# A macaron block (mixture, state space, mixture) on one core: other mixture groups, results in the sorted rows, the drive product in halves, the bias as bf16, and another written order

## The chip, the cores and the metric

The kernel runs on one core of one Trainium2 chip. The time is the device time of one execution, in microseconds; less is better. Six units matter. TensorE (PE) multiplies matrices. VectorE (DVE), ScalarE (ACT) and GpSimd (POOL) work element by element. SyncE (SP) starts the transfers (DMAs) of a hardware queue, GpSimd those of a software queue, whose rows are picked by an index.

## The reference

The input is two sequences of 2048 tokens with 128 features. Three steps are added to it in turn. A "mixture" is a mixture of 32 experts, four for each token, plus a shared network; both mixtures have the same weights. The "state space" is a selective scan with 256 channels and 16 states.

```python
x = x + 0.5 * _L0_ffn_ref(_layernorm(x, axis=-1), ...)
x = x + _L0_attn_ref(_layernorm(x, axis=-1), ...)
x = x + 0.5 * _L0_ffn_ref(_layernorm(x, axis=-1), ...)

# mixture
scores = softmax(flat @ router_w.T + router_bias)
topk_scores, topk_idx = jax.lax.top_k(scores, 4)          # then normed to a sum of 1
h = silu(einsum('nd,ehd->neh', flat, gate_w)) * einsum('nd,ehd->neh', flat, up_w)
expert_out = einsum('neh,edh->ned', h, down_w)
out = (sel * topk_scores[:, :, None]).sum(axis=1)         # sel: the four chosen
out = out + silu(flat @ sgate_w.T) * (flat @ sup_w.T) @ sdown_w.T

# state space
x_proj, z = split(x @ W_in + b_in, 2);  u = silu(x_proj)
Bm, Cm = split(u @ W_x + b_x, 2);       dt = softplus(u @ W_dt + b_dt)
def step(h, inp):
    h = h * exp(dt_t[..., None] * A) + (dt_t * u_t)[..., None] * B_t[:, None, :]
    y_t = einsum('bds,bs->bd', h, C_t) + D_param * u_t
    return (h, y_t)
return (y * silu(z)) @ W_out + b_out
```

## The kernel before

The 4096 tokens are eight blocks of 512 (four tiles of 128 each), blocks 0 to 3 for one sequence and 4 to 7 for the other. Everything is in fp32 unless said otherwise.

**State space.** Blocks go one after the other (`state_space`, L1281). A block's opening works out u, z, B, C, dt and dt times u (`dtu`). Then there are 16 states, each with these steps. SP spreads a row of B over the partitions (`bs`). GpSimd multiplies `dtu` by it into `hst`, both halves of the channels (2 x 512) in one instruction (`drive`, L1456). ScalarE makes two decays `da` (`decay`, L1468). TensorE spreads a row of C (`c`, L1480). VectorE runs two scans in place on `hst`, one for each half (`scan`, L1494), and multiplies by C (`times_c`, L1507). TensorE adds the transposed result to `y` (L1271). Four `hst` buffers are in turn. At the end of a block `project` (L1566 to 1584) multiplies by W_out; its first matmul for each tile has a single row of ones (`ones_row`) against the row of the bias (`bout`), both fp32.

**Mixture.** `mixture(li, gi)` (L649) does one group of blocks of a layer. Layer one has the groups (0), (1), (2, 3) and (4, 5, 6, 7); layer two has (0, 1, 2, 3), (4, 5), (6) and (7). VectorE's routing finds for each token its four experts and a row for each choice, so that rows of one expert lie together in tiles of 128. GpSimd scatters the normed tokens to these rows in DRAM (`scatter`, L916, one DMA for a tile and a choice). Then the experts work on a "quad", four tiles at a time. SP loads the rows (`xs`) and the weights (`wt`), TensorE transposes (L1066), multiplies by gate and up (`gate_up`, L1076) and down (`down_q`, L1104), ScalarE copies and applies silu, VectorE multiplies, and SP stores the results (`ys`). GpSimd gathers each token's four results (`gather`, L1197), TensorE sums them with their weights (`weighed`, L1230), VectorE adds the sum to x.

A group works on a fixed number of tiles, `SURE`: 32, 48 or 80 for one, two or four blocks; so a layer has 8 + 8 + 12 + 20 = 48 quads. Tiles beyond that are worked in a branch (`more`) only where the routing needs it. A group of one block has one tile for each expert, so its weights are the experts in order: it reads them from the inputs in three pieces, gate, up and down (`take`, L1016), and the first group also writes them out side by side (`lay`) as `w_dram`. Larger groups take each tile's weights from `w_dram` by the routing's list (`fetch`, L1038). Sorted rows lie in one DRAM buffer for each size of group, results in others, two for each size used in turn. All are cleared with zeros at the start (`clear_rows`, L466): rows fully, results beyond the fixed tiles. That is 52 and 24 stores of 256 KB.

**Order.** Each step is an operation with an engine, a list of buffers read and written, and a function that emits its instructions. `ORDER` (L47) is a written list of the numbers of these operations; the kernel emits them in exactly this order, and each engine runs its own in the order of emission. So an engine that waits at one operation holds up all its later ones. ScalarE's activation tables are loaded where the next operation in the order needs the other set (`tables`, L413). On GpSimd, from the third of a row of scatters or gathers on, a small memset (`pause`, L408) stands ahead of each.

Of the kernel before, what the change touches and what calls it, by code (L numbers as in the profile page):

```python
# [8 lines left out]
F32 = mybir.dt.float32  # L9
# [21 lines left out]
SURE = {1: 32, 2: 48, 4: 80}  # L31
# [4 lines left out]
GROUPS = (((0,), (1,), (2, 3), (4, 5, 6, 7)), ((0, 1, 2, 3), (4, 5), (6,), (7,)))  # L36
# [11 lines left out]
0 10 108-112 20 113 9 19 2 528 8 3 529 114-120 14 121 123 21 23 25 16 24 15 17-18 530-531 31 1 122 124-125 22 126-128  # L48
131 27 132-133 537 532 29 533 326 538-539 134 534-535 11 129-130 536 41 540-544 135 148 150 144 149 146-147 143 145
142 140 139 141 170 13 12 151 153 545-548 138 549 34 37 327 35 39 32 137 551 328 186 550 552-553 152 155 28 554 26 154  # L50
202 136 171 329 156-157 38 218 36 188 40 30 555 158 33 558 159 161 160 162 169 163-165 556 330 166-167 559 185 557 201
331 174-175 594 560 168 190 596 6 191 176-177 187 172 561 217 206 332 233 207 178 333-335 595 179 597 336-337 180-181
338 222 4 192 182 223 193-194 183 208-209 195-196 204-205 211 857 212 197 265 210 219 339 224 340 213 225 5 226 342
598 341 343 599-600 173 344 601 220 856 184 92 198-199 203 249 238 189 602 227 562 592 234 239 604 228-229 281 603 605
855 574 568 7 200 214 606 345 266 215 608 230 607 609 270 231 271 610 587 221 858 236 254 611 346 250 252 282 582
859-860 612 255 251 283 349 613 240 614 575 570 237 615 243 284 616 861 241-242 244 268 245 286 618 253 287 272-274
256 267 257 216 617 258 619 235 285 620-621 624 622 246 626 247 623 269 862-863 866 591 564 625 627 275 297 628 589
276-277 629 278-279 291-292 565 43 293 584 590 967 969 248 350 288-290 69 968 95 232 970-971 347-348 389 388 973 259
52 59 260 972 105 261 572 975 974 871 351 977 567 976 569 262 978 263 979 981 45 980 60 982 294 352 295 983-984
369-372 573 64 566 373 67 375 588 374 280 377 379 91 66 376 378 380 578 872 864-865 873 876 381 583 383 382 384 581  # L60
403 867 877 48 874 868 296 878 107 875 264 42 879-880 869 68 46 585 870 881-883 886 885 50 57-58 61 100 44 51 884 887
63 888 580 385 402 593 571 891 62 563 386 889 47 579 65 98 55 586 75 577 576 49 353 368 367 354 357 365-366 362 364
358-359 355 360-361 363 890 892-893 356 894-895 82 387 390-391 56 392 54 393 395-396 394 298 397 401 96 300-301
404-405 415 418 409 314 419 313 53 429 306 305 308-309 320 406 417 416 423 410-411 424 407 299 408 432-433 443 425
398-399 457 302 446 896 431 430 412-413 307 319 445 434-435 899 436 414 447 437 303 420 438-439 310 421-422 444 458
304 311 460 630 322 312 461 316 426 321 448 427 315 459 323 317 633 400 90 471 318 428 634 449-450 798 903 451-453
324-325 70 1432-1433 465-467 462 631 463 440-441 1434 464 106 635-637 454 485 101 632 455 468-469 900 473 644 474-475
917 479-481 1435-1436 638 1439 639 1440 934 442 658 472 97 645 487 640-641 913 960 642 470 486 456 488 647 489 648 952
476 102 919 477-478 1437 661 490 672 1438 928 491 646 906 923 908 493-494 662 72 914 933 492 905 499 495 675 907 922
916 926 909 912 924 659 649-651 904 932 910 686 482 676 83 652-653 927 918 931 929 921 654 94 483 936 925 915 920 911  # L70
930 961 1458 643 1459 74 1460 1452-1453 1461-1462 93 1463 1454 660 673 99 496-497 1455-1456 655 700 1441-1442 964 943
656 1445-1446 1448-1449 687 674 701 663 1450-1451 1457 680-682 664-665 715 1447 484 959 938 666 677 667-668 1466 657
688 669 678 689-690 670 679 985 1470 498 987 1468 683-684 1467 1471 703 1469 714 1472-1473 951 940 76 1464 986 988
1476 1478 704 1479 1465 728 717 1486 1496 1477 1481 691 73 1480 692-693 718 705-706 1506 694 702 1482 695-696 707 671
716 1475 1488 731-732 1489 1483 697 897 955 966 1487 898 698 742 965 729 85 708 699 709-710 79 719-720 1490 756 1491
1485 1492-1493 730 1516 721 1498 1484 757 711 1500 944 941 722 1474 712 736 1495 733 1497 1499 685 1526 1501-1503 953
939 1510 1508 737 1507 723 1504 734 724-725 735 1509 738 726 1511 942 937 745 71 743 1512 739-740 949 80 1513 758 744
759 746 1518 950 1519 1494 946 1517 956 1443 760 1521 1505 770 1522 1444 771 747 1520 989 991 1536 947 748-749 508 784
764-765 935 1527 785 766 990 954 992 962 945 750 993 995 713 727 761 751 772 762 1515 1528 1537 963 500 958 948 957
752 81 1523 763 994 753 1524 1529 786 507 1530 996 773 1531-1532 1514 741 1533 754-755 774 1538 1541 1546 775 767 776  # L80
768 1556 502 1547 1540 777 787 1539 503 501 1542 1054 1040 788 1525 1535 1548 789-791 1557 516 1543 997 1068 778-780
521 792 1545 793-794 1055 1053 999 781 1039 1550 998 1000 1067 769 1081 1534 1549 782 1551-1552 795-796 1056 1042 1057
504 1558 1041 1553 1043 1559 1058 505 1059 797 1060 783 506 1069 1061-1063 1070-1071 1082 1047 1084 1048-1049 510
1561-1562 514 523 509 1085 511 77 1566 1064-1065 1072-1074 1044-1045 1095 1075 1109 1046 1555 88 1076 1544 1083 1096
1123 522 1567 517 1568 1050 1077-1078 515 524 1051 1066 901 1079 1098-1099 1124 1560 1563 1112 1571 1576 512 1110 1089
1113 1569 1090 513 1086 1097 1126 89 799 1091 1572 1087 1565 518 1088 1570 525 1127 1100 1573 1554 1101 1577 519-520
1102 526-527 1636 1578 1637 1111 1092 1001 1137 1093 1581 1002 1114 1638 1579 1588 1115 1128-1129 1116 1103 1586 1104
1130 1639 1105 800 84 1052 1080 1117 1125 1640 78 1118 1106 86 1138 87 803 821 1094 1107 1140 1119 1141 1587 1003 1120
807 1005 806 1596 1131 820 1564 1121 1582 1591 1132-1133 1151 808 1643 1152 1139 1597 1641 1606 1574 1644 1142 1642
902 1143 1580 1134 1656 1575 1589 1135 1598 1657 1144 1136 1592 1165 1601 1004 802 1599 1583 1662 1658 1663 1607 1006  # L90
1659-1660 1166 1664 1608 1122 1661 1585 1590 1602 1593 1154 1616 1155 1179 1600 1665 1611 1666 1584 1609 1645 1153
1145 1603 1146 1180 1617 1649 1612 1147 1610 1613 1646 1193 1604 1650 1652 1108 1159 1168 822 801 1653 1651 1160 1169
# [225 lines left out]
def macaron_kernel(  # L318
# [162 lines left out]
    for (li, gi), b in results.items():  # L481
        if b.t is not None and not b.writers:
            clear_rows(b, SURE[len(GROUPS[li][gi])] // SQ)
# [1172 lines left out]
```

## Time and profile before

| | us |
|---|---|
| median of 7 runs | 1267.98 |
| lowest and highest of them | 1263.65 and 1272.78 |
| the profiled execution | 1272.94 |
| its span, first to last instruction | 1271.2 |
| busy: POOL | 973.3 |
| busy: PE | 969.2 |
| busy: DVE | 823.2 |
| busy: ACT | 784.8 |

The busy time of an engine is an average over stages with different limits, so it is read by stretches of the span. A stretch's row gives for each engine its busy time and the number of its instructions, then the granted clock of TensorE as a share, the mean busy share of the 16 DMA engines and what they moved. In the slices, each digit is the busy share of a fortieth of the span in tenths (9 is 90% or more). A row of the groups gives line, engine, operation, what is written from what, shapes and number; then the busy time of all, the mean of one in ns; then how long the engine had been idle just before them and what ended most of that. TensorE shows an fp32 matmul as two records.

### The profile page before, as it was taken

The numbers are of one execution on the slowest core, as the hardware profiler recorded it, in microseconds if no ns is written. First come the engines' busy times: TensorE is split into PE (matmuls) and PEld (weight loads), VectorE is DVE, ScalarE is ACT, GpSimd is POOL, SyncE is SP. The second block draws the span as 40 slices with busy tenths as digits, with TensorE's granted clock in tenths as the row PEclk, the third lists the DMA queues.
The fourth block names the chain that finished last, engine by engine and source line by source line (L and its number), as shares of the span: only waits on it lengthen the run. The fifth ranks groups of instructions, "written<-read, shape, count | busy, mean of one in ns | idle before, by whom it ended". The sixth has DMA issues, their size and how long they took to land. (4 is left out here: it accounts for less than half of the span.)

```text
span 1271.2 us, 19402 instructions
## 1 busy us (share of the span) xinstructions
PE 969.2 (76%) x5848; PEld 769.6 (61%) x5848; DVE 823.2 (65%) x1643; ACT 784.8 (62%) x1532; POOL 973.3 (77%) x1043
## 2 busy tenths in 40 slices
PE   3777775778798978877677665668898889778776
PEld 2556564566767767564555444446777877676664
DVE  7652452166576999899989999989788632312221
ACT  4342343576789999577879735776687737424442
POOL 3876578288858775798989879998886867588686
PEclk9998987899999999688888877989899989979997
DMA  9797767488978554222232212232788978677842
GB/s 317 228 301 242 254 199 218 152 267 279 307 215 248 152 165 145 75 66 72 82 86 64 78 45 88 95 115 82 230 263 256 293 226 260 163 214 195 218 112 68
DMA packets 253513, 226.85 MB, mean 178 GB/s; under 512 B 24513, under 2 KB 218690, under 8 KB 253378
## 3 DMA queue, kind: packets, MB, share of 16 engines
q1 hardware_dynamic: 236994, 191.67, 49.6%
q0 software_dynamic: 16384, 33.59, 9.2%
q8 instruction: 59, 0.97, 0.3%
q14 instruction: 76, 0.62, 0.2%
HBM read 154.65 MB, written 70.52 MB: 177 GB/s over the span
## 5 line engine op out<-in xcount | busy, mean ns | idle before, releaser
L1456 POOL TENSOR_TENSOR hst<-dtu,bs 128x1024 f32<-128x1024 f32 x128 | 302.3, 2367 | 58.4 <-ACT st L1519 11.2
L1197 POOL DMA_INDIRECT yg<-ys,idx x256 | 246.5, 963 | 108.1 <-PE sum L1230 39.3
L1076 PE MATMUL gu<-xT,wt 128*128 128x128 f32 x1536 | 221.7, 297 | 50.9 <-issue 23.5
L1076 PEld LDWEIGHTS gu<-xT,wt 128*128 128x128 f32 x1536 | 205.5, 210 | 82.6 <-issue 39.6
L1494 DVE TENSOR_TENSOR_SCAN hst<-da,st,hst 128x512 f32<-128x512 f32 x192 | 240.2, 1272 | 17.5 <-POOL hst L1456 8.8
L916 POOL DMA_INDIRECT xs<-xn,idx x192 | 189.4, 987 | 75.8 <-issue 38.3
L1468 ACT ACTIVATE da<-dt,a 128x512 f32<-128x512 f32 x256 | 174.8, 690 | 74.0 <-DVE hst L1494 63.5
L1094 DVE TENSOR_TENSOR h<-sgq,gu 128x256 f32<-128x256 f32 x192 | 77.9, 417 | 201.5 <-ACT sgq L1088 88.8
L1271 PEld LDWEIGHTS y<-ident,hst 128*128 128x128 f32 x1024 | 133.0, 155 | 76.2 <-issue 48.7
L415 ACT ACT_TABLE_LOAD x130 | 166.8, 1283 | 4.1 <-ACTq L1139 1.0
L1271 PE MATMUL y<-ident,hst 128*128 128x128 f32 x1024 | 149.6, 296 | 18.5 <-DVE hst L1507 17.4
L1507 DVE TENSOR_TENSOR hst<-hst,c 128x1024 f32<-128x1024 f32 x128 | 154.9, 1210 | 13.1 <-PE c L1480 5.3
L1088 ACT ACTIVATE sgq<-gu 128x256 f32<-128x256 f32 x192 | 71.1, 383 | 137.3 <-PE gu L1076 73.5
L1104 PE MATMUL oq<-wt,h 128*128 128x128 f32 x768 | 109.6, 289 | 20.0 <-issue 12.3
L1104 PEld LDWEIGHTS oq<-wt,h 128*128 128x128 f32 x768 | 100.7, 202 | 34.2 <-issue 20.3
L1480 PE MATMUL c<-cm,pick 128*128 128x512 bf16 x128 | 54.7, 428 | 79.7 <-DVE hst L1507 75.7
L409 POOL MEMSET pad<- 128x256 bf16 x336 | 110.1, 328 | 0.2
L1113 ACT COPY yq<-oq 128x512 f32<-128x512 f32 x96 | 55.7, 585 | 81.4 <-PE oq L1104 38.7
L1230 PEld LDWEIGHTS sum<-yg,dg 128*128 128x128 f32 x512 | 71.4, 209 | 38.5 <-issue 17.8
L1230 PE MATMUL sum<-yg,dg 128*128 128x128 f32 x512 | 77.9, 299 | 20.5 <-issue 11.3
L1222 ACT ACTIVATE dg<-ident,wk 128x128 f32<-128x128 f32 x256 | 80.9, 393 | 13.3 <-PE sum L1230 13.3
L1069 ACT COPY xT<-pt_x 128x512 f32<-128x512 f32 x96 | 55.8, 584 | 48.0 <-PE pt_x L1066 15.5
(154 smaller groups left out, 1519.2 us busy)
## 6 DMA issues: line engine op xcount, KB each, us to landing
wt<-w_dram SPq DMA_DIRECT2D x256, 192.0 KB
bs<-bd SPq DMA_DIRECT2D x128, 256.0 KB
xs<-xs SPq DMA_DIRECT2D x96, 256.0 KB
ys<-yq SPq DMA_DIRECT2D x96, 256.0 KB
xs<-zero SPq DMA_DIRECT2D x52, 256.0 KB
wt<-in_gate_w SPq DMA_DIRECT2D x64, 128.0 KB
wt<-in_up_w SPq DMA_DIRECT2D x64, 128.0 KB
wt<-in_down_w SPq DMA_DIRECT2D x64, 128.0 KB
```

The source lines that it names most:

```text
L409: pool(nc.gpsimd.memset(pad, 0.0))
L415: nc.scalar.preload_act_table_set(name)
L916: nc.gpsimd.indirect_dma_start(out=xs_b.t, out_offset=bass.IndirectOffsetOnAxis(ap=route["idx"][:, i * TB + t, k : k + 1], axis=0), in_=xn ...
L1076: nc.tensor.matmul(gu.t[:, j, s, :], wt.t[:, s, j * H : (j + 1) * H], xT.t[:, s0 + s, :], start=True, stop=True,)
L1104: nc.tensor.matmul(o.t[:, s, :], h.t[:, s, :], wts[s // 2].t[:, s % 2, 2 * H :], start=True, stop=True,)
L1197: nc.gpsimd.indirect_dma_start(out=yg.t[:, k, :], out_offset=None, in_=ys_b.t, in_offset=bass.IndirectOffsetOnAxis(ap=route["idx"][:, i * ...
L1230: nc.tensor.matmul(sm_.t, dg.t[:, k, :], yg.t[:, k, :], start=(k == 0), stop=(k == TOPK - 1),)
L1271: nc.tensor.matmul(y[:, t, k * P : (k + 1) * P], src[:, k, t * P : (t + 1) * P], ident.t, is_transpose=True, start=start and k == 0 and t ...
L1456: nc.gpsimd.tensor_tensor(h.t[:, :, 1:], dtu.t, bs.t.unsqueeze(1).to_broadcast([P, ND, T]), ALU.mult)
L1468: nc.scalar.activation(da.t, dt.t[:, k, :], AF.Exp, scale=a_t.t[:, k, s : s + 1])
L1494: nc.vector.tensor_tensor_scan(h.t[:, k, 1:], da.t, h.t[:, k, 1:], 0.0 if ini else st_sb[:, k, s : s + 1], ALU.mult, ALU.add,)
L1507: nc.vector.tensor_tensor(h.t[:, :, :T], h.t[:, :, 1:], cb.t.unsqueeze(1).to_broadcast([P, ND, T]), ALU.mult,)
```

## The change

It has five parts.

- Groups: layer one is (0), (1, 2, 3), (4, 5, 6, 7), layer two (0, 1, 2, 3), (4, 5, 6), (7). A group of three blocks works on 68 tiles, so a layer has 8 + 17 + 20 = 45 quads. The single group of layer two reads its weights from `w_dram` in one piece for two experts (`again`) rather than from the inputs in three.
- Results: for groups of three and four blocks they are stored over the sorted rows that they come from; only groups of one block have a buffer for results. Rows are cleared with 12 + 20 + 24 stores and results with 4.
- GpSimd's product for a state is two instructions of 512 elements, one for each half, and a scan depends on its own half.
- Bias: at the start VectorE splits it into three bf16 rows whose sum stands for the fp32 value, in partitions 0, 32 and 64 of a tile of zeros (`bo3`). In `project` a bf16 matmul of 128 rows of ones with this tile replaces the fp32 one.
- `ORDER` is another list: 4327 operations in place of 4340.

```diff
-SURE = {1: 32, 2: 48, 4: 80}
+SURE = {1: 32, 3: 68, 4: 80}
-GROUPS = (((0,), (1,), (2, 3), (4, 5, 6, 7)), ((0, 1, 2, 3), (4, 5), (6,), (7,)))
+GROUPS = (((0,), (1, 2, 3), (4, 5, 6, 7)), ((0, 1, 2, 3), (4, 5, 6), (7,)))
 ORDER = """
...
@@ buffers in DRAM
             if n not in rows:
                 rows[n] = dram_buf(f"xs{n}", [slots(blocks) * P, D])
-            same = [k for k in results if len(GROUPS[k[0]][k[1]]) == n]
-            if len(same) < 2:
-                results[li, gi] = dram_buf(f"ys{n}{len(same)}", [slots(blocks) * P, D])
-            else:
-                results[li, gi] = results[same[len(same) % 2]]
+                if n == 1:
+                    results[n] = dram_buf(f"ys{n}", [slots(blocks) * P, D])
+                else:
+                    results[n] = Buf(t=rows[n].t)
...
-    for (li, gi), b in results.items():
-        if b.t is not None and not b.writers:
-            clear_rows(b, SURE[len(GROUPS[li][gi])] // SQ)
+        if n == 1:
+            clear_rows(results[n], SURE[n] // SQ)
...
+    bo3 = kept("bo3", [P, D], BF16)
+
+    def parts():
+        left = const.tile([1, D], F32, tag="bo_left", name="bo_left")
+        nc.vector.memset(bo3.t, 0.0)
+        nc.vector.tensor_copy(bo3.t[0:1], bout.t)
+        nc.vector.tensor_tensor(left, bout.t, bo3.t[0:1], ALU.subtract)
+        mid = const.tile([1, D], BF16, tag="bo_mid", name="bo_mid")
+        nc.vector.tensor_copy(mid, left)
+        nc.vector.tensor_copy(bo3.t[32:33], mid)
+        nc.vector.tensor_tensor(left, left, mid, ALU.subtract)
+        nc.vector.tensor_copy(bo3.t[64:65], left)
+
+    op("dve", 1.0, parts, r=[bout], w=[bo3])
...
@@ scatter
-                        w=[xs_b] if first else [],
+                        w=([xs_b] if fixed else [xs_b, ys_b]) if first else [],
...
@@ weights of a group of one block
+                    def again(e=q * SQ + s0, wt=wt):
+                        nc.sync.dma_start(wt.t, w_routed.t[e : e + 2].rearrange("e p f -> p e f"))
+
                     op(
                         "sp",
-                        1.4,
-                        take,
-                        r=[] if lead else [sl_b],
+                        1.4 if lead else 0.6,
+                        take if lead else again,
+                        r=[] if lead else [sl_b, w_routed],
...
@@ a state
-            def drive(bs=bs, h=h):
-                pool(
-                    nc.gpsimd.tensor_tensor(
-                        h.t[:, :, 1:], dtu.t, bs.t.unsqueeze(1).to_broadcast([P, ND, T]), ALU.mult
-                    )
-                )
-
-            op("pool", 2.35, drive, r=[dtu, bs], w=[h])
+            halves = [Buf() for _ in range(ND)]
+            for k in range(ND):
+
+                def drive(k=k, bs=bs, h=h):
+                    pool(nc.gpsimd.tensor_tensor(h.t[:, k, 1:], dtu.t[:, k, :], bs.t, ALU.mult))
+
+                op("pool", 1.2, drive, r=[dtu, bs], w=[halves[k]], p=[h])
...
-                op("dve", 1.2, scan, r=[das[k], st_b[s]], w=[h])
+                op("dve", 1.2, scan, r=[das[k], st_b[s]], w=[halves[k]], hold=[h])
...
-            op("dve", 1.15, times_c, r=[cb], w=[h])
+            op("dve", 1.15, times_c, r=[cb, *halves], w=[h])
...
@@ project
-                        ones_row.t,
-                        bout.t,
+                        ones_bf.t,
+                        bo3.t,
```

## The prediction

> **What bounds the kernel now.** I read the page's shares and slices first.
>
> ```profile
> PE 969.2 (76%) x5848; PEld 769.6 (61%) x5848; DVE 823.2 (65%) x1643; ACT 784.8 (62%) x1532; POOL 973.3 (77%) x1043
> DVE  7652452166576999899989999989788632312221
> DMA  9797767488978554222232212232788978677842
> ```
>
> No engine is full, and what is full changes. DMA is busy at both ends and VectorE (DVE) in the middle, so a sum over the whole span says little. I therefore cut the span at the first scan of each block's state space (by the timeline of the scans: 264, 393, 478, 555, 629, 700, 796, 898 us) and at the last scan (1014), and asked for each stretch.
>
> ```profile
> core 0: us, PE busy (x) PEld busy (x) DVE busy (x) ACT busy (x) POOL busy (x), PEclk, DMA share, GB/s
> 0.00:264.00 264.00, 183.37 (x974) 140.15 (x974) 112.23 (x457) 107.68 (x217) 167.35 (x262) 0.89 0.76 240
> 264.00:393.00 129.00, 107.05 (x752) 90.69 (x753) 84.44 (x122) 102.38 (x192) 101.60 (x94) 0.97 0.86 266
> 393.00:478.00 85.00, 75.46 (x489) 58.11 (x488) 76.45 (x104) 79.13 (x153) 65.51 (x47) 0.98 0.62 182
> 478.00:555.00 77.00, 64.05 (x341) 48.60 (x340) 68.46 (x85) 60.09 (x113) 57.02 (x35) 0.80 0.32 94
> 555.00:629.00 74.00, 53.01 (x297) 40.33 (x295) 69.73 (x95) 57.92 (x102) 67.68 (x48) 0.86 0.27 76
> 629.00:700.00 71.00, 52.18 (x279) 37.61 (x280) 66.70 (x95) 57.94 (x121) 63.10 (x42) 0.88 0.29 77
> 700.00:796.00 96.00, 59.98 (x296) 44.73 (x297) 91.56 (x169) 51.22 (x100) 83.07 (x63) 0.79 0.24 71
> 796.00:898.00 102.00, 73.51 (x380) 50.68 (x377) 94.51 (x155) 70.99 (x118) 92.34 (x81) 0.92 0.31 98
> 898.00:1014.00 116.00, 102.22 (x751) 90.03 (x750) 91.17 (x166) 90.95 (x152) 91.86 (x90) 0.96 0.88 272
> 1014.00:1271.00 257.00, 198.40 (x1306) 168.71 (x1304) 67.99 (x201) 106.48 (x270) 183.76 (x287) 0.91 0.65 183
> ```
>
> Call the rows head, S0 to S7 and tail. In S1 to S6 the stretch is only 4 to 9 us longer than its busiest engine: there an engine's sum is the time. S0 has 22 us over PE with DMA at 0.86, S7 14 us. Head and tail have 81 and 59 us over their busiest engine: DMA and a chain of steps set them. The durations:
>
> ```profile
> L1456 POOL TENSOR_TENSOR hst<-dtu,bs 128x1024 f32<-128x1024 f32 x128 | 302.3, 2367 | 58.4 <-ACT st L1519 11.2 <-PE y L1271 10.7 <-DMA bs<-bd 9.5
> L1426 POOL TENSOR_TENSOR dtu<-dt,u 128x512 f32<-128x512 f32 x16 | 20.6, 1288 | 1.3
> L1424 POOL TENSOR_TENSOR w<-w,ea 128x512 f32<-128x512 f32 x16 | 20.3, 1271 | 26.2 <-ACT w L1419 26.1
> L415 ACT ACT_TABLE_LOAD x130 | 166.8, 1283 | 4.1 <-ACTq L1139 1.0 <-PEq L1644 0.8
> L409 POOL MEMSET pad<- 128x256 bf16 x336 | 110.1, 328 | 0.2
> L1480 PE MATMUL c<-cm,pick 128*128 128x512 bf16 x128 | 54.7, 428 | 79.7 <-DVE hst L1507 75.7
> L1568 PE MATMUL ps_o<-bout,onesr 1*128 1x128 f32 x64 | 17.3, 354 | 7.9 <-DVE cm L1372 4.8 <-DVE pos L814 1.2 <-DVE z L1561 0.7
> ```
>
> **The change part by part.**
>
> *Groups.* 96 quads (four tiles through an expert) become 90: 8+8+12+20 to 8+17+20 per layer. From the groups, a quad costs PE 221.7/96 + 109.6/96 + 62.4/96 = 4.1 us, ScalarE (ACT) 71.1/96 + 55.8/96 + 55.7/96 = 1.9 and DVE 0.8; so PE loses 25 us and ACT 11, wherever the quads stand.
>
> *Results in place.* 76 clearing stores (52+24 issues) become 60: 16 x 0.26 MB. In the written order 62 stand before S0's first product now, 36 then. The price is a wait: layer two's scatters into the group-of-four's rows must follow all 64 gathers of layer one's. In the new order the last 15 of those stand in S5, before the 12 scatters of that stage; now 11 gathers stand before 19 scatters there. Nothing else on GpSimd (POOL) is pushed, so I cost it at nothing. Without that cover it would cost the 15 gathers, 14 us.
>
> *Weights in layer two's single group.* Sixteen 384 KB reads replace 96 pieces of 128 KB (two single groups), whose SP issues cost 0.45 to 0.9 us each in the chain. That chain also waits 5.13 us for a gate piece and 3.63 us for an up piece. I take -9 in the tail, between 0 and -20 (some 40 fewer issues x 0.5).
>
> *Product in halves.* No 128x512 product of this kind is in the trace. Below, half of 2367 is 1183 (two halves can't do fewer elements); above, L1426's 1288. I take 1275, the mean of the three such lines: 128 x (2 x 1.275 - 2.367) = +23 us of POOL (0 to +27). In return a scan waits for one half: the scans' idle time on the product is 10.9 us in all, so the gain is between 0 and 11. I take 3; most of these stretches are short of DVE, not of the product.
>
> *Bias.* 64 records of 354 ns (17.3 us) become 32 bf16 matmuls. Upper bound 428 ns as in L1480, lower a quarter of it (128 of 512 columns), 107; I take 0.21 with its weight load, so PE loses 10.6 us, between 3.6 and 13.9, four per block. DVE sets S3 to S6, so it is worth 1 to 2 us in all.
>
> *Order.* Counting the written orders between the same marks, before > after (the product counted whole or in halves):
>
> | | scatters | gathers | pauses | quads | table loads | clears |
> |---|---|---|---|---|---|---|
> | head | 104>64 | 16>16 | 114>78 | 20>13 | 15>9 | 62>36 |
> | S0 | 24>38 | 29>32 | 21>59 | 17>12 | 22>24 | 14>24 |
> | S1 | 0>26 | 18>16 | 5>3 | 7>6 | 16>24 | 0 |
> | S2 | 0 | 12>8 | 0>1 | 4>14 | 10>18 | 0 |
> | S3-S6 | 64>49 | 53>56 | 28>0 | 0 | 40>40 | 0 |
> | S7 | 43>51 | 0 | 21>15 | 20>16 | 23>21 | 0 |
> | tail | 21>28 | 128>128 | 147>156 | 28>29 | 4>4 | 0 |
>
> With 0.98 per scatter, 0.96 per gather, 0.33 per pause:
> - Head, POOL -52. The first group's last quad ends at 133 us, its first weighted sum starts at 180, its last sum ends at 199, block 0's first product starts at 260. Until 133 I see little change (33.0 MB queued by then, 32.0 after). From 133 to 180 the DMAs queued fall from 17.3 to 11.2 MB: 47 > 30 us. 180 to 199 stays. The 65 us from 199 to the first scan at 264 hold 9 quads and 40 scatters of other groups between block 0's own steps; then 2 quads and no scatter stand there. They lie between 65 (no gain) and 24 (block 0's own instructions one after the other, by their rows); I take 34, near the lower end, since nearly all that stood between has left. So 133+30+19+34 = 216: **-48**, between -17 (only the DMAs give) and -73 (all goes as the bytes, 51 of 70 MB with scatters and gathers counted).
> - S0, POOL 102+35 = 136 (14 scatters 14, 38 pauses 12, gathers 3, halves 5), because the group of four is now routed and scattered here, in front of block 1's products. PE, counted alike, is 134, DVE 124. With the slack cut from 22 to 13, since 8 MB less is moved: 149, **+20**.
> - S1, POOL 66+26 = 92, plus its old slack 6 = 98, **+13**; S2, ten quads more on PE (41, less 14 for weighted sums, shared work and a gate's part that leave): 64+27 = 91, plus 5 as in S4 = 96, **+19**.
> - S3 to S6, DVE -19 (two blocks' routing less, and quads' and shared products), **-18**; S7, PE 102+6 with its old slack, **+6**; scans that start on a half, **-3**.
> - Tail: POOL +10, PE -6, neither full: 0, less 9 for weights, **-9**.
>
> Sum -48+20+13+19-18+6-3-9 = -20. The profiled run took 1272.94 us (span 1271.2 and 1.7 around it), so 1253; the median of the runs shown is 5 lower than that run: **1248 us**.
>
> Table loads go from 130 to 140, 13 us of ACT, inside S1 and S2, where ACT reaches 85 and 86, under POOL's and PE's 92 and 91. The load's row has 4.1 us idle ahead of all 130, and at 241.65 us the next activation starts right at a load's end. The Trainium skill (ScalarE: Activation LUTs, What ACT_TABLE_LOAD costs) gives a load 1283 ns, as here, plus a drain of 1380 ns at each switch. By it, an estimate, the ten would cost 27 us instead of 13; the trace shows no such drain.
>
> **The rivals.**
> - *The order moves work, it does not save it (slower).* If block 0's own chain keeps the head at 240 (-24), POOL's 35 scatters and 33 pauses ahead of block 1's first product stay in full. S0 keeps its slack (136+22 = 158), S1 is 98, S2 keeps its 9 (100): +65. With -18, +6, -3 and -9 that is +17: 1285. It decides where the head gives less than 41. For it: S0 already had POOL at 0.79 of its time. Against: 40 scatters, 7 quads and 26 clears leave the head.
> - *All of it pays.* The head goes by bytes (-73), S0 to S2 sit 4 us over their busiest engine like S3 and S4 (140+96+95, +40), S3 to S7 -12, halves -11, tail -20: -76, so 1192. For it: DMA at 0.76 in the head. Against: the chain up to 133 is hardly touched, and no stretch with three engines above 0.8 sits so close (S7: 14 us).
> - *Gain and loss cancel*: the head gives just those 41: 1264 to 1272, no change.
> - *Switching costs more than the load's row.* A second 1.3 us for each of the ten loads, which lifts ACT to the bound of S1 and S2: 1248+13 = 1261. Nothing in the rows speaks for it. This is the drain of the Trainium skill above.
>
> **How the numbers follow.** Forecast 0.50 (1225 to 1263), all pays 0.17, dearer switching 0.03, cancelling 0.09, slower 0.21. Range 1203 to 1287: it leaves out about half of the second rival's cases and half of the first's. Faster by over 0.3% (about what can be told from no change here) means under 1264: 0.50+0.17+0.03 = 0.70; same 0.09; slower 0.21.
>
> **What would show it.** Right: first product of block 0 near 212 us rather than 260; stretch S0 near 150 us with POOL above 0.85; S2 near 95; scans of S3 to S6 some 18 us shorter in sum; halves at 1.25 to 1.3 us each; the bias's matmuls near 0.1 us. Wrong: a head above 235 us, gaps of DVE over 30 us before block 1's first scan, or a tail above 265 us because all 17 quads of the group of three now wait for block 6.

## The result, and the profile after

The changed kernel takes 1262.8 us (median of 27 runs), the kernel before 1269.65 us (69 runs beside it): 0.996 of the time, 95% interval 0.9945 to 0.9975. It is faster, by 5 to 7 us where 20 were forecast (1248 us). The profiled execution took 1260.56 us with a span of 1258.8; that of the kernel before 1272.94 with 1271.2. On two other chips the sign is the other one, 1.030 (1.027 to 1.032) and 1.028 (1.023 to 1.033); the first experiment is about that.

Cut at the same marks as before (first scan of each block, last scan), the stretches of the changed kernel are these. The columns are those of the prediction's second fence.

```profile
core 0: us, PE busy (x) PEld busy (x) DVE busy (x) ACT busy (x) POOL busy (x), PEclk, DMA share, GB/s
0.00:182.00 182.00, 122.62 (x665) 91.59 (x666) 71.56 (x279) 75.32 (x154) 115.28 (x184) 0.84 0.82 254
182.00:356.00 174.00, 134.44 (x765) 100.00 (x764) 114.26 (x259) 115.90 (x221) 134.18 (x166) 0.86 0.51 162
356.00:466.00 110.00, 83.43 (x480) 61.73 (x479) 79.44 (x98) 85.38 (x148) 96.75 (x90) 0.90 0.54 168
466.00:552.00 86.00, 75.02 (x544) 62.77 (x544) 72.64 (x89) 78.62 (x140) 49.79 (x42) 0.98 0.71 220
552.00:630.00 78.00, 54.12 (x300) 40.91 (x301) 71.18 (x98) 52.88 (x102) 71.83 (x64) 0.87 0.29 77
630.00:698.00 68.00, 48.43 (x257) 33.13 (x255) 65.91 (x86) 61.55 (x120) 63.98 (x56) 0.93 0.28 79
698.00:785.00 87.00, 53.18 (x251) 40.14 (x251) 84.42 (x151) 53.08 (x103) 77.63 (x67) 0.74 0.23 71
785.00:877.00 92.00, 68.08 (x353) 46.18 (x353) 84.08 (x116) 69.23 (x115) 83.63 (x74) 0.93 0.26 80
877.00:1004.00 127.00, 106.53 (x768) 90.02 (x768) 97.44 (x190) 86.36 (x144) 100.82 (x108) 0.97 0.77 239
1004.00:1259.00 255.00, 193.82 (x1273) 164.10 (x1273) 66.75 (x194) 106.62 (x270) 194.54 (x303) 0.92 0.62 187
```

The head is 82 us shorter (264 to 182). S0 is 45 us longer, S1 25, S2 9; S3 to S6 together are 18 shorter, S7 is 11 longer, the tail 2 shorter: -12. In S0 the sums of the engines came out as forecast (POOL 134 and PE 134 against 136 and 134). What failed there is how long a stretch lasts over such sums: S0 takes 174 us with no engine above 135. In S1 GpSimd's sum is 97 us against 92, in S2 TensorE's 75 against 91.

From the page of the changed kernel, the lines that answer to those shown of before:

```profile
DVE  7412359657556769888999999989896553121211
DMA  9887959842123868733231321223489867886622
L1471 POOL TENSOR_TENSOR hst<-dtu,bs 128x512 f32<-128x512 f32 x256 | 323.1, 1282 | 74.0 <-ACT st L1531 17.8
L414 ACT ACT_TABLE_LOAD x140 | 179.6, 1283 | 4.2 <-PEq L1656 0.8
L408 POOL MEMSET pad<- 128x256 bf16 x312 | 102.2, 328 | 0.2
```

The half products take 1.282 us each, 21 us more of GpSimd in all (forecast 1.275 and 23). The ten table loads more have no idle time of their own: 4.2 us ahead of all 140. The bias in the view of groups of instructions:

```profile
L1580 PE MATMUL ps_o<-bo,ones 128*128 128x128 bf16 x32 | 7.3, 228 | 3.7 <-DVE z L1573 2.8 <-ACTq L1152 0.7 <-DVE ea L1423 0.2
```

7.3 us instead of 17.3, so -10.0 where -10.6 was costed. DVE's slices show the hole that the head's gain fell into: the digits 5, 7, 5, 5 from the ninth to the twelfth slice (252 to 378 us) hold S0's second half, where no scan runs from 303 to 356 us.

### The profile page after: what moved, and what is told of

The parts are those of the page before. It is cut to its first block, busy times and chain, and to the rows that moved or that the text cites. A ratio compares the mean times of both kernels' runs of the same rounds, so it can differ in the third digit from the quotient of the medians.

```text
span 1258.8 us, 18884 instructions
## 1 busy us (share of the span) xinstructions
PE 939.7 (75%) x5642; PEld 730.6 (58%) x5642; DVE 807.7 (64%) x1550; ACT 784.9 (62%) x1510; POOL 988.4 (79%) x1146
## 5 line engine op out<-in xcount | busy, mean ns | idle before, releaser
L1471 POOL TENSOR_TENSOR hst<-dtu,bs 128x512 f32<-128x512 f32 x256 | 323.1, 1282 | 74.0 <-ACT st L1531 17.8
L1210 POOL DMA_INDIRECT yg<-xs,idx x224 | 216.9, 968 | 71.5 <-issue 40.1
L1089 PE MATMUL gu<-xT,wt 128*128 128x128 f32 x1440 | 197.4, 289 | 32.6 <-issue 8.0
L1089 PEld LDWEIGHTS gu<-xT,wt 128*128 128x128 f32 x1440 | 181.0, 200 | 49.5 <-issue 16.2
L414 ACT ACT_TABLE_LOAD x140 | 179.6, 1283 | 4.2 <-PEq L1656 0.8
L1284 PE MATMUL y<-ident,hst 128*128 128x128 f32 x1024 | 154.1, 303 | 28.8 <-DVE hst L1519 28.5
L1107 DVE TENSOR_TENSOR h<-sgq,gu 128x256 f32<-128x256 f32 x180 | 71.5, 418 | 154.1 <-issue 80.0
L1117 PE MATMUL oq<-wt,h 128*128 128x128 f32 x720 | 104.1, 291 | 23.6 <-DVE h L1107 11.2
L1101 ACT ACTIVATE sgq<-gu 128x256 f32<-128x256 f32 x180 | 64.5, 384 | 91.6 <-PE gu L1089 46.4
L1117 PEld LDWEIGHTS oq<-wt,h 128*128 128x128 f32 x720 | 93.3, 202 | 35.0 <-DVE h L1107 17.5
L1243 PE MATMUL sum<-yg,dg 128*128 128x128 f32 x512 | 80.2, 303 | 34.9 <-DMA yg<-xs,idx 14.2
L408 POOL MEMSET pad<- 128x256 bf16 x312 | 102.2, 328 | 0.2
```

Of the source, the lines that this page charges most:

```text
L408: pool(nc.gpsimd.memset(pad, 0.0))
L414: nc.scalar.preload_act_table_set(name)
L1089: nc.tensor.matmul(gu.t[:, j, s, :], wt.t[:, s, j * H : (j + 1) * H], xT.t[:, s0 + s, :], start=True, stop=True,)
L1117: nc.tensor.matmul(o.t[:, s, :], h.t[:, s, :], wts[s // 2].t[:, s % 2, 2 * H :], start=True, stop=True,)
L1210: nc.gpsimd.indirect_dma_start(out=yg.t[:, k, :], out_offset=None, in_=ys_b.t, in_offset=bass.IndirectOffsetOnAxis(ap=route["idx"][:, i * ...
L1243: nc.tensor.matmul(sm_.t, dg.t[:, k, :], yg.t[:, k, :], start=(k == 0), stop=(k == TOPK - 1),)
```

## The experiments

**1. Both kernels again, each with its trace, on chips where they take other times.** No edit.

> The changed kernel itself once more, beside the other runs of this call, because chips differ in the stretches that DMA sets. Expected from its runs: a ratio of 0.996 to the kernel before. If the ratio is 0.985 or lower here, then the change's worth hangs on the chip, and variants are to be read against this run alone.

1231.4 us beside 1196.8: 1.0298 (1.0273 to 1.0323). Neither 0.996 nor a ratio of 0.985 or lower came: the worth differs from chip to chip, but here the change loses. On the next chip both were traced.

> The kernel before once more, for its trace on the chip of this call. On three chips it has taken 1270, 1322 and 1197 us, the changed kernel 1261 on the first and 1231 on the third. Theory, the change trades time that DMA sets for time that GpSimd and the order set: from chip to chip only head, S7 and tail move, S0 to S6 stay within 4 us each of 129, 85, 77, 74, 71, 96, 102 (634 in all). Rival, all stretches scale with the chip: S0 to S6 move by the same per cent as the whole.

> The changed kernel on the same chip as the run above. Theory: S0 to S6 within 4 us each of 174, 110, 86, 78, 68, 87, 92 (695 in all, 61 more than the kernel before); the head is 40 to 90 us shorter, the more so the slower the chip's transfers are, and the sign of the whole follows from the head: slower than the kernel before where that one's head is under about 240 us, faster where it is above 265. Rival: one ratio on all chips.

1198.7 us (0.9997) and 1232.4 us (1.0278, 1.0229 to 1.0328). Stretches on that chip, first four of the kernel before (head, S0, S1, tail), then two of the changed kernel (head, tail):

```profile
0.00:230.00 230.00, 174.48 (x974) 132.59 (x974) 112.18 (x456) 106.64 (x215) 168.40 (x262) 0.92 0.87 274
230.00:356.00 126.00, 108.75 (x753) 93.74 (x754) 86.20 (x122) 103.15 (x195) 102.42 (x94) 0.95 0.88 274
356.00:439.00 83.00, 74.64 (x487) 58.04 (x486) 76.24 (x104) 78.92 (x152) 65.38 (x46) 0.97 0.65 186
970.00:1198.00 228.00, 185.89 (x1310) 161.78 (x1308) 67.29 (x200) 106.24 (x270) 184.45 (x287) 0.94 0.72 207
```

```profile
0.00:176.00 176.00, 120.24 (x659) 91.75 (x659) 70.92 (x278) 73.98 (x152) 114.75 (x183) 0.84 0.84 260
988.00:1228.00 240.00, 187.21 (x1278) 159.73 (x1277) 67.02 (x195) 105.69 (x270) 202.80 (x315) 0.92 0.66 200
```

S0 to S6 move little from chip to chip, as the theory had it (634 and 629 us before, 695 and 695 after). But the same program before is 73 us shorter here, 34 in the head and 29 in the tail, and the changed one 31. It is not what transfers take: a packet of 512 bytes takes 28 ns by the mean in both traces of before, and one of 2 KB 104 and 105. Nor is it TensorE's granted clock, 0.902 and 0.903. So the theory's reason fell; two other things differ. First, waits that end on nothing that the trace shows ("issue", "remote"). The longest of the waits of the kernel before, for ScalarE and for VectorE, on the chip of the first profile:

```profile
ACT sgq L1088 <- remote: 25.6, 9, 8.4
ACT xT L1069 <- issue: 15.2, 4, 9.8
DVE h L1094 <- issue: 84.8, 50, 8.6
DVE x L988 <- remote: 12.1, 2, 6.5
```

and all that there are of the same program on the later chip:

```profile
ACT bc L1330 <- issue: 1.9, 1, 1.9
ACT sc L719 <- issue: 1.6, 1, 1.6
DVE h L1094 <- issue: 0.2, 1, 0.2
```

Summed over ScalarE and VectorE they are 220 us against 4 for the kernel before, 209 against 3 for the changed one. This sum is a mark of the two sorts of trace and not the time lost, because the label is rough: the 9.5 us ahead of `h` at 53.9 us in the changed kernel ends where the `sgq` that it needs ends, at 53.88, and `h` starts 33 ns after its `sgq` by the median in both traces of before. A stricter count is of `sgq` itself: after its last `gu` matmul has ended and with ScalarE free, it starts over 0.5 us late 25 times of 192 in the first trace of before (25 us in all), and never in the later one. Second, SP's register moves, 29 ns by their median: 30 of 258 last over 100 ns and up to 511 in the first trace of before, none in the second (42 at most). With fused register operations counted too, 29 of the 35 over 100 ns stand within three or more indirect transfers that start at most 2 us apart, where 47% of all such instructions stand; in the changed kernel's first trace it is 21 of 26, with 37% there.

Call these times stops, with the sum of the labelled waits as their mark. Every trace here has either 200 us of it or more, or 4 or less: the profiles of the result and the runs beside a kernel before of 1270 and 1322 us have stops, those beside 1197 to 1199 don't. Each chip was used at one time only, those with stops before the others, so the chip and the time are not told apart; "a chip with stops" says no more than that.

So the account is: without stops the change costs 30 us (1198.2 to 1228.2 in span). With them the kernel before is 73 us longer and the changed one 31. 30 - 42 = -12, the result. That the 73 us are the stops' is argued from where both stand (170 of the 220 us of labelled waits and 63 of the 73 us are in head and tail); no run took the stops alone away.

**2. The pauses.** The clear between two indirect transfers was the first suspect for GpSimd's time.

```
-                o.pause = row > 2
+                o.pause = False
```

> The changed kernel without the small memsets ahead of GpSimd's scatters and gathers. Theory 1, GpSimd's queue sets stretches S0, S1 and the tail: in the trace two gathers in a row start 1.44 us apart with a memset between and 1.29 us without, so 0.15 us goes for each of 312; in S0, S1 and the tail that is 0.15 x 218 = 33 us, the time falls to about 1230 us. Rival, TensorE and the transfers set the tail and block 1's late mixture sets S0 and S1: at most 8 us go, 1255 us or more.

> The kernel before without the same memsets. Theory 1: 0.15 us for the 147 in the tail, 22 us, and little elsewhere: about 1247 us. Rival (TensorE and transfers set the tail): at most 8 us go, 1261 us or more.

On a chip with stops: 1395.4 us, 1.0999 (1.0956 to 1.1041) of the kernel before, and 1403.6, 1.1058 (1.1018 to 1.1097). Both theories were wrong: ScalarE's and VectorE's stops grow from 209 to 429 us in the one and from 220 to 372 in the other.

```
-    pad = const.tile([P, 256], BF16, tag="pad", name="pad")
+    pad = const.tile([P, 64], BF16, tag="pad", name="pad")
```

> The changed kernel with each pause between GpSimd's indirect transfers cut from a 128x256 clear (0.328 us) to a 128x64 clear, which I take to last 0.13 to 0.25 us; 312 of them. Without any pause the same kernel took 1395 us. Theory 1, GpSimd's queue sets the tail and block 1's start, and any instruction between two transfers does: spacing 1.44 becomes 1.25 to 1.36, the tail loses 13 to 30 us and S0 with S1 3 to 10 us, 1225 to 1247 us. Rival, the pause's length is what the other engines need: 1275 us or more, between this kernel and the one without pauses.

1409.5 us beside 1322.05, 1.0689 (1.0639 to 1.0739), stops 414 (265 with full pauses on that chip, in `a_take`): the rival held. The short pause takes 0.165 us, and transfers then start 1.29 us apart by the median, against 1.44 with the full one and 1.27 with none. That fits the distance as what counts, and not that something stands between. The same line with 512, and then two pauses for one until block 0's first product:

> The changed kernel with each pause a 128x512 clear instead of 128x256 (about 0.6 us instead of 0.328). The trace of the changed kernel has 41 stops of over 3 us in which an engine waits for nothing that is shown, and 36 of them fall where indirect transfers go at 0.5 to 0.9 per us. Theory 1, dense indirect transfers hold the other engines: with a transfer every 1.7 us these stops shrink, the head is 10 us or more shorter, S0 about the same, and the tail, which GpSimd's queue sets, 156 x 0.28 = up to 44 us longer: 1270 to 1305 us. Rival, the pause's length matters to GpSimd's queue alone: the head as before, S0 up to 16 us and the tail 44 us longer, 1310 to 1325 us.

> The changed kernel with two pauses instead of one, but only ahead of block 0's first product, where GpSimd's queue is not what is waited for (64 scatters and 16 gathers in 182 us); the rest as it was. Theory 1 (dense indirect transfers hold the other engines): stops such as the 12.2 us at 49 and the 9.5 us at 54 us shrink, block 0's first scan is 8 to 20 us earlier, and the run 4 to 20 us faster than the changed kernel. Rival (the first group waits for its weights and rows, and the stops are elsewhere the same): within 4 us either way.

Both ran on a chip without stops (1 and 0 us), so they could not show whether longer pauses shorten them; they show what pauses cost. 1295.5 us, +64 to the changed kernel beside it, 34 of them in the tail (238 to 272) and 11 in S0; and 1259.2, +28, all in the head (177 to 204). With two pauses the first group's gathers start at 141.4 us instead of 116.6, in both kernels right behind the scatters of the group of three in GpSimd's queue: without stops that queue sets when they start, and with it the head. Last, on a chip without stops, no pauses at all, on top of the kernel `b_both` of part 5:

> The same without the pauses between GpSimd's indirect transfers. Without them the kernel before took 1.106 of its time on a chip where ScalarE and VectorE stop for 220 us in all with nothing that the trace shows, and SP's 29 ns register moves last over 100 ns in 35 of 514 cases; on the chips of the last two calls these stops sum to 0 to 4 us and no such move lasts over 100 ns. Theory, the pause pays only for these stops: on a chip without them this kernel is faster than the one with pauses by what GpSimd's queue gets back (336 pauses, of which some 150 in the tail at 0.15 us each and as many ahead of block 0 and block 1: 20 to 50 us, 0.96 to 0.985 of the kernel before); on a chip with them it takes 1.09 to 1.11. Rival, the pause is needed on every chip: 1.05 or more on a chip without stops too.

1178.1 us, 0.9827 (0.9797 to 0.9858), against 1198.2 with the pauses: the theory held. Without stops the pause costs this kernel 1.7%. This is the fastest kernel of the study, on a chip without stops. On one with stops it wasn't tried; by the first two runs a kernel without pauses loses 10% there.

**3. What makes S0 174 us.** GpSimd's timeline of the changed kernel, first profile (start, length, what, idle before):

```profile
242.76 0.98 POOL L1210 DMA_INDIRECT yg<-xs,idx  x1 [1.69 <-DMA xs<-yq]
244.05 0.95 POOL L1210 DMA_INDIRECT yg<-xs,idx  x1 [0.30 <-issue]
245.00 0.33 POOL L408 MEMSET pad<- 128x256 bf16 x1
245.49 0.95 POOL L1210 DMA_INDIRECT yg<-xs,idx  x1 [0.17 <-issue]
...
341.09 0.96 POOL L925 DMA_INDIRECT xs<-dtu,idx  x1 [0.17 <-issue]
342.08 1.28 POOL L1437 TENSOR_TENSOR w<-w,ea 128x512 f32<-128x512 f32 x1
```

From 242.8 to 342 us, 32 gathers, two products and 33 scatters without a gap of 2 us, one transfer every 1.44 us: 0.95, 0.33 for the pause, and 0.165 that no busy row counts. Only then block 1's opening gets its turn. In the first edit 32 of these scatters issue nothing:

```
-                        scatter,
+                        (lambda: None) if lent and i < 2 else scatter,
```

> The changed kernel without the 32 scatters of layer one's group of four that stand ahead of block 1's first product (its first two blocks' tokens; their sorted rows stay as cleared, so that part of the result is left out). In the changed kernel GpSimd goes from 243 to 342 us without a gap (32 gathers, 33 scatters, one every 1.44 us), and only then takes block 1's opening, whose operand has been ready since 329.6 us. Theory 1, GpSimd's queue holds block 1: the opening's first product there starts at its operand, 12 us earlier or more (up to 32 x 1.44 = 46 if the steps before it, which stand in the written order beside the scatters, move up too), so block 1's first scan is at 344 us or before instead of 356, and the run takes 1235 to 1252 us. Rival, block 1 is late by itself (the 17 quads of the group of three and its opening steps): first scan at 350 or later, 1256 to 1264 us.

1292.3 us, 0.9776 (0.9736 to 0.9817). S0 167 us, against 173 and 176 in two kernels beside it (`a_halfg`, `a_take`) that leave S0 as it is: 6 to 9, between the rival's 6 at most and Theory 1's 12 or more. The second edit takes away quads 9 to 16 of the group of three:

```
+            none = li == 0 and gi == 1 and q > 8
+
+            def quad(eng, cost, fn, none=none, **k):
+                return op(eng, cost, (lambda: None) if none else fn, **k)
...
-            op(
+            quad(
```

> The changed kernel in which layer one's group of three computes 9 of its 17 quads (the other eight are left out with their reads and writes, so their tokens' expert results are wrong); scatters, gathers and sums stay. With the group's quads at 134 to 238 us in the changed kernel's trace, eight quads are some 49 us of them. Theory 1, block 1 is late because its group of three is: its gathers start 30 to 49 us earlier, but GpSimd then still runs 32 gathers and 33 scatters before block 1's first product (99 us), so S0 is 125 to 150 us long instead of 174. Rival, GpSimd's queue alone holds block 1 (32 gathers and 33 scatters wait on other things): S0 165 us or more.

1216.0 us, 1.0132 beside 1.0278 for the changed kernel. S0 161 us, 13 less: between the two. Three kernels, S0 cut at the first of block 1's gathers, and at the opening's first product:

```profile
176.00:235.00 59.00, 51.99 (x405) 46.33 (x405) 52.51 (x72) 56.04 (x99) 36.30 (x30) 1.00 0.90 274
235.00:336.00 101.00, 76.83 (x357) 51.06 (x356) 59.78 (x180) 51.94 (x109) 85.90 (x127) 0.83 0.33 112
336.00:350.00 14.00, 4.22 (x9) 1.99 (x8) 2.30 (x8) 8.92 (x17) 12.81 (x11) 0.66 0.21 77
```

is the changed kernel on the chip without stops, then with eight quads less,

```profile
175.00:223.00 48.00, 31.85 (x185) 24.93 (x184) 46.18 (x57) 31.93 (x58) 36.44 (x31) 0.79 0.47 146
223.00:322.00 99.00, 76.73 (x357) 51.03 (x356) 59.92 (x180) 51.59 (x108) 85.33 (x127) 0.84 0.31 102
322.00:336.00 14.00, 4.09 (x9) 1.97 (x8) 2.32 (x8) 8.92 (x17) 12.79 (x11) 0.65 0.24 77
```

and with 32 scatters less (this one on a chip with stops), where GpSimd then waits for block 1's operand:

```profile
203.00:264.00 61.00, 53.18 (x404) 47.54 (x404) 52.61 (x72) 55.99 (x99) 36.19 (x29) 0.97 0.89 264
264.00:350.00 86.00, 65.81 (x315) 44.46 (x315) 52.99 (x165) 49.56 (x105) 44.26 (x63) 0.88 0.31 108
350.00:370.00 20.00, 11.97 (x47) 7.11 (x45) 10.33 (x24) 7.84 (x18) 14.11 (x12) 0.68 0.15 52
349.70 1.70 POOL L1439 TENSOR_TENSOR w<-w,ea 128x512 f32<-128x512 f32 x1 [33.95 <-ACT w L1434]
```

So S0 is 59 + 101 + 14. The 59 wait for the group of three's last results, and with half its quads gone still 48, because 29 half products of block 0 stand ahead of the gathers in GpSimd's queue and come at the pace of the scans (36 us of work); there the first gather starts 0.14 us behind the last of them. The 101 are that queue: 86 of work and the short gaps. Without the 32 scatters block 1's own sums and opening take 86 instead. Two limits lie close together, and taking either away shows the other. Both at once was not tried.

**4. The tail.** First, half of the gathers of layer two's group of three:

```
-                        gather,
+                        (lambda: None) if li == 1 and gi == 1 and k > 1 else gather,
...
-                            yg.t[:, k, :],
+                            yg.t[:, k % few, :],
```

> The changed kernel with half of the gathers of layer two's group of three left out (24 of 48 in the stretch after its last quad; the sums read the first two of a token's four expert rows twice, so that part of the result is left out; products and sums stay as many). Theory 1, GpSimd's queue sets the tail: 24 x 1.44 = 35 us less on it, tail 220 to 235 us instead of 255, 1228 to 1243 us. Rival, the last group's eight quads (weights, gates, in the order written) set it: tail 250 or more, 1256 to 1264 us.

1281.2 us, 0.9693 (0.9651 to 0.9735). The tail of this kernel, and of the one without the scatters beside it, whose layer two is as in the changed kernel:

```profile
1025.00:1273.00 248.00, 195.25 (x1272) 164.79 (x1273) 66.01 (x194) 107.56 (x271) 160.78 (x250) 0.91 0.61 184
```

```profile
1019.00:1289.00 270.00, 200.98 (x1272) 171.07 (x1273) 66.66 (x194) 106.40 (x270) 195.23 (x303) 0.89 0.58 176
```

22 us less (20 to 35 by Theory 1, 5 at most by the rival) for 34.5 less of GpSimd's busy time: its queue sets much of the tail, not all. Second, the weights of the single group as before:

```
-                        take if lead else again,
-                        r=[] if lead else [sl_b, w_routed],
+                        take,
+                        r=[] if lead else [sl_b],
```

> The changed kernel with layer two's single group reading its weights as the kernel before did, in 48 pieces of 128 KB out of the inputs instead of 16 reads of 384 KB out of the copy. The prediction's term: the tail gets 9 us longer (0 to 20), 1272 us. Rival, GpSimd's queue sets the tail (from 1022 to 1214 us it has no gap above 7 us: a gather or scatter every 1.44 us): 1260 to 1266 us.

> The changed kernel with the weights of layer two's single group in 48 pieces of 128 KB out of the inputs, this time beside the changed kernel itself on the same chip. The prediction's term: 9 us slower than it (0 to 20). Rival, GpSimd's queue sets the tail: within 4 us of it.

The first had no changed kernel beside it (1298.4 us, 0.9821; a tail of 274 against 270). The second did: 1230.7 against 1232.4, tails of 238 and 240. The rival held; the 9 us aren't there on a chip without stops.

**5. Parts alone.** In the kernel before the product in halves, and in the changed kernel the whole product again:

```
-            op("pool", 2.35, drive, r=[dtu, bs], w=[h])
+            halves = [Buf() for _ in range(ND)]
+            for k in range(ND):
...
+                op("pool", 1.2, drive, r=[dtu, bs], w=[halves[k]], p=[h])
```

> The kernel before with GpSimd's product in two halves alone, the second right behind the first in the written order, nothing else moved. Prediction's price: +23 us of GpSimd's busy time, against at most 11 us of scans that waited for a product, so about -3 us where VectorE sets the stretch (1264 to 1268). Rival, GpSimd sets most stretches: +8 to +20 us.

> The changed kernel with the product whole again, at the place of the first of its two halves (in 11 states the two scans are put in the other order for it). If halves are worth what the prediction took (-3 us net), 1263 + 3 = 1266. If GpSimd is the bound in S0 and S1 and waits for the product don't matter, about 6 us less: 1257. If scans that start on a half are what fills VectorE between the gathers, 10 us or more slower: 1273.

On a chip with stops: 1.0056 (1.0031 to 1.0082), 5 to 7 us slower in the old order; 0.9989 (0.9964 to 1.0014) for the new order without halves, against 0.996 with them, so 4 us for the halves there, with an interval of about 4 either way. The scans that carry a state in, in the kernel before, with halves alone, in the changed kernel with the product whole, and in the changed kernel:

```profile
L1494 DVE TENSOR_TENSOR_SCAN hst<-da,st,hst 128x512 f32<-128x512 f32 x192 | 240.2, 1272 | 17.5 <-POOL hst L1456 8.8
L1499 DVE TENSOR_TENSOR_SCAN hst<-da,st,hst 128x512 f32<-128x512 f32 x192 | 240.6, 1273 | 14.2 <-ACT da L1473 6.3
L1502 DVE TENSOR_TENSOR_SCAN hst<-da,st,hst 128x512 f32<-128x512 f32 x192 | 240.0, 1273 | 42.5 <-POOL hst L1464 28.8
L1506 DVE TENSOR_TENSOR_SCAN hst<-da,st,hst 128x512 f32<-128x512 f32 x192 | 240.1, 1274 | 45.7 <-POOL hst L1471 35.1
```

In the old order halves do shorten the scans' idle time (17.5 to 14.2), and the kernel is slower all the same. The longer waits of the changed kernel come with the new order and groups, with whole products too. Then results in the sorted rows for the groups of two and four, alone and with the bf16 bias:

```
-            if len(same) < 2:
+            if n > 1:
+                results[li, gi] = results[same[0]] if same else Buf(t=rows[n].t)
+            elif len(same) < 2:
```

> The kernel before with one part of the change alone: the results of its groups of two and four blocks are written over their sorted rows, so 16 clears (4.2 MB) go, the order is otherwise the same. If the head goes by bytes, as the prediction's second step had it, 4.2 MB at the head's 240 GB/s are 17 us: a head of 247 to 255 us and 8 to 17 us faster. Rival, block 0's own chain and the order around it set the head: 0 to 4 us.

> The kernel before with the two parts of the change that need no new order: the output bias as one bf16 product (the prediction: 1 to 2 us), and results of the groups of two and four written over their sorted rows (16 clears less, by themselves 0.9986 of the kernel before). Theory: 0.997 of the kernel before, between 0.995 and 1.000, on either sort of chip; the groups, the halves and the order then carry the rest of the change's gain and loss. Rival, the parts pay only together with the new order: 0.999 or more.

0.9986 (0.997 to 1.0002) and 0.9992 (0.9971 to 1.0013), both without stops. The first rival holds: 4.2 MB less in the head are worth nothing measurable there (a head of 226 us, in the other chip's trace of the kernel before 230). The second result, 0.9992, fits its rival and the upper part of its theory's range, and with this interval the bias's 1 to 2 us can't be told from nothing. Whether the clears pay where there are stops was not tried.

## Why the prediction was right or wrong

By its own steps, in us; the last column is the chip without stops (1198.2 to 1228.2). It goes by the scans' exact times and can differ by 1 from rows cut at whole us.

| step | forecast | first profile | without stops |
|---|---|---|---|
| head | -48 | -82 | -54 |
| S0 | +20 | +45 | +48 |
| S1 | +13 | +25 | +27 |
| S2 | +19 | +9 | +14 |
| S3 to S6, with the halves' -3 | -21 | -18 | -22 |
| S7 | +6 | +11 | +7 |
| tail | -9 | -2 | +11 |
| sum | -20 | -12 | +30 |

- **The head.** The -48 is near the -54 of the chip without stops. It was added up from nothing until the first group's last quad, 17 from there to its first sum, nothing in the sums and 31 behind them; there the four are 13, 8, 2 and 31. So the main term, other groups' work between block 0's own steps, is right, and that the first two make up for each other is luck. On the first chip 28 more go: the old head is 34 us longer there than on the later chip and the new one 6. Of the old head's 34, 16 lie before the first group's last quad. The waits with no shown end were in the rows, and the prediction didn't ask about them.
- **S0 failed**, at "with the slack cut from 22 to 13": a busy sum of GpSimd plus a slack. The sum was right and the rule was not. GpSimd can't spread its 134 us over S0, because its queue is in order: 59 us at the pace of scans and quads, then 101 of transfers that block 1 waits behind. The prediction named those 35 scatters, in its slower rival, and priced them there at 9 us; experiment 3 shows that they, and behind them block 1's own 86 us, set the second half of S0.
- **S1 and the tail failed** on a price: "0.98 per scatter, 0.96 per gather, 0.33 per pause" leaves out the gap of 0.165 us ahead of a transfer that follows a pause (0.30 ahead of one that follows a transfer), so 1.44 a transfer instead of 1.29. With the gaps under 0.45 us added, GpSimd fills 105 of 109 us in S1, 84 of 87 in S5, 92 of 92 in S6 and 226 of 239 in the tail (chip without stops). The tail was put down as "neither full: 0, less 9 for weights"; the 9 aren't there (experiment 4), and GpSimd's filled time there was 207 of 227 us in the kernel before, so 19 more of it make a tail that is 11 longer.
- **S2** is 5 to 10 us shorter than forecast because TensorE's sum was too large: the added quads raise its busy time by 11 us (64 to 75), where the prediction had 27. So TensorE isn't S2's bound, as it was forecast to be; ScalarE is busier, at 79 of 86 us.
- **S3 to S6, S7, product and bias** came out within 3, 5, 2 and 1 us. In S3 to S6 GpSimd, its gaps counted, is as full as VectorE, and was so before the change (73 of 74 us, 68 of 71, 91 of 96, 102 of 102), so "DVE sets S3 to S6" was half of it.
- **Scans that start on a half, -3**: -4 with 4 either way in the new order, which is consistent, but +5 to +7 in the old one, although the scans waited less there. That the 21 us of GpSimd's time that two halves cost outweigh the earlier start is the likely reason, and not shown apart.
- **Table loads** cost their 1283 ns and no more. The rule of the Trainium skill (ScalarE: Activation LUTs, What ACT_TABLE_LOAD costs) of 1380 ns of drain at each switch isn't borne out: 4.2 us of idle time ahead of 140 loads. Behind a load the next instruction starts within 0.1 us in 128 of 140 cases.
- **The rivals.** "The order moves work, it does not save it" has the right outcome on a chip without stops, not by its condition: the head gave 54, over the 41 that it asked for, and S0 and S1 took 75.
- **Two slips.** The sign for the bias, "near 0.1 us", isn't the 0.21 of the prediction's own sum (measured 0.228). And "no stretch with three engines above 0.8 sits so close (S7: 14 us)" passes over S1 of the kernel before, which has three engines at 0.88 and more and is 6 us longer than the busiest.

The direction was right on the first chip for a reason that the sum doesn't hold: -12 is +30 of order and groups and -42 that goes with the stops, which have no term in the sum. That a head 34 us better than forecast met 25 and 12 us of S0 and S1 is luck. Of the forecast's miss of 15 us at the median, 8 are the sum (-20 for -12); the rest is that the median was put 5 under the profiled run and came out 2 above it.

What stops the engines on some chips stays open. Shown are the two sorts of traces, that the labelled waits grow as indirect transfers come closer together (from 252 us in `a_whole` to 429 without pauses on one chip, from 265 in `a_take` to 414 with short ones on another), and that without stops a kernel without pauses is faster. That it is the transfers' descriptors that hold other engines' control instructions was not tried apart. Nor is it shown why the new order loses less to them; 40 fewer scatters in a head where TensorE, ScalarE and VectorE depend on each other step by step fits, and is only argued.

## What to carry to other kernels

Add up an in-order engine by the distance from one start to the next, not by its busy time: with the gaps of 0.165 us ahead of its transfers GpSimd filled 0.95 to 1.00 of S1, S6 and the tail on the chip without stops, while its busy share there read 0.85 to 0.91. A stretch whose head is "wait for the others" and whose rest is one queue lasts as long as the two in turn, whatever the sums say. And before a stretch's slack is put down to order or transfers, sum the waits that end on nothing shown, and run the same program on a second chip: here that was 73 us, six times the effect.

## What the hardware showed that was not expected

- One program took 1197, 1199, 1270 and 1322 us on different chips, with granted clocks of 0.87 to 0.91. Between the traces at 1199 and 1270 packets of one size take the same and the clock is 0.903 and 0.902; ScalarE's `sgq` starts over 0.5 us late 25 times in the slower one and never in the other.
- A clear of 0.328 us between two indirect transfers is worth 10% on the one sort of chip and costs 1.7% on the other. With a clear of 0.165 us the transfers start 1.29 us apart, nearly as with none (1.27), and the kernel takes 1.069 of the kernel before on the first sort.
- GpSimd's product over 128x512 takes 1282 ns against 2367 for 128x1024: splitting costs 0.2 us a pair.
